# A gated recurrence of 512 steps: the product with wh_W from three bf16 parts, r and z in one fp32 product

## The chip, the cores and the metric

The kernel runs on one core of a Trainium2 chip. The metric is the time of one execution on the device in microseconds; where several runs are named, their median. PE (TensorE), VectorE (DVE), ScalarE (ACT), GpSimd (POOL) and SyncE (SP) are the engines of that core; PEld is TensorE's loading of weights, which can overlap its matmuls.

## What is computed

The input x has 8 sequences of 512 steps with 512 values, h0 is (8, 512). With T = 512 steps in order:

```python
def step(h, x_t):
    fused = sigmoid(concatenate([x_t, h], -1) @ w_W + w_b)
    hidden_state, output_state = split(fused, 2, -1)          # r, z
    memory_state = x_t @ wx_W + wx_b + hidden_state * (h @ wh_W + wh_b)
    h_new = output_state * h + (1.0 - output_state) * tanh(memory_state)
    return h_new, h_new
_, hs = scan(step, h0, swapaxes(x, 0, 1))
return x + swapaxes(hs, 0, 1)
```

Everything is fp32. The products with x_t do not depend on h; the three products with h (r's and z's lower half of w_W, and wh_W, each 512 x 512) do, so a step cannot begin before the step ahead of it has given h.

## The kernel before, in words

**Layout.** The 512 hidden values lie as 4 chunks k of 128 partitions. Chunks 0 and 1 are half A of the state, chunks 2 and 3 half B; a tile hT of one half holds both its chunks. For a product, the state of a chunk is the stationary operand (32 columns: 4 steps of a group times 8 sequences, of which 8 are this step's) and the weights are the moving one. The output's 128 partitions are four groups j of 32 rows: a matmul with `to[32 * j : 32 * j + 32]` uses a quarter of the array's columns, and four of them, one for each j, can run side by side. One matmul call in fp32 leaves two LDWEIGHTS and two MATMUL records.

**Banks of a step.** Three PSUM tiles, double buffered by groups of GS = 4 steps: A (192 columns: h, z and r of half a), B (128: r and h of half b) and C (64: z of half b). "Half a" and "half b" are here halves of each group's 128 output columns, which become half A and half B of the new state. TensorE takes the steps' products in the order `ORDER` (line 27; the digit is the chunk k of the state), each item being four matmuls (line 344). Behind them come 7 matmuls of the x side (line 351, `take(later, 7)`): products of x with wx for later groups, 192 columns each, which do not depend on the recurrence. The first index j is turned by 7 each step (`turn`, line 352), so that the four groups j, which get 2, 2, 2 and 1 of the seven, take turns in having one less. In the first five steps the x side is `prefill` (384 columns a matmul); at the end of the run, from about step 501, it is used up.

**VectorE and ScalarE, in program order of a step** (lines 426 to 451): VectorE transposes 32 x 32 blocks out of PSUM, ScalarE takes sigmoid and tanh, and scans do the arithmetic. `turn_r(0)`, `turn_h(0)`, `turn_z(0)`, then `memory(0, 0)` and `memory(0, 1)`: for each chunk a scan of 16 elements, which makes r * (h wh_W + wh_b) + x-part, and a tanh. Then `turn_r(1)`, `turn_h(1)`, `update(0, 0)`, `turn_z(1)`, `update(0, 1)`: the update is a scan of 24 elements (three slots for each sequence: h, tanh, new h), and its output in slot 2 is the new state that the next step's A0 (chunk 0) and A1 (chunk 1) load as weights. Then `memory(1, ...)`, `update(1, ...)`, whose output A2, A3 and so on load, and a ScalarE copy of each half's new state into slot 0 of the tile. Each engine works in this order; a wait blocks what stands behind it on that engine. `idle` (lines 400 and 504) are tiny memsets on VectorE.

**Beside it**: `turn_x` transposes the x-part of the memory state, `spread` and other ScalarE copies prefill banks A, B and C with the x-parts, POOL makes sums of x (`x_sum`) and adds x to the new state for the output (`add`, two of them a step), SP loads x and stores the output in blocks of 16 steps.

**Start.** SP loads wx (4 x 768 KB), wa (4 x 384 KB) and wb (1152 and 384 KB). VectorE makes weight sums `tw` for the x side (line 277), two of them ahead of step 0.

The next lines are the functions that the change touches.

## Time and profile before

| | |
|---|---|
| three runs | 1674.72 us median, 1672.09 to 1675.40 |
| profiled execution, its span | 1670.8 us |
| PE busy | 1659.0 us (99%), 56238 records |
| PEld busy | 1637.5 us (98%), 56238 records |
| VectorE busy | 1090.5 us (65%), 9387 instructions |
| ScalarE busy | 1029.9 us (62%), 5822 instructions |
| POOL busy | 301.9 us (18%), 1281 instructions |
| DMA | 31.40 MB, mean 19 GB/s |

How to read the lines that follow. Busy shares are unions of record times; matmuls are pipelined, so that records of one engine overlap, and a record is longer than the time after which the next one can start. A line of the timeline has start and length in us, the engine, the source line, the operation, output tile <- input tiles, the shape (partitions x elements; 128*32 is 128 rows by 32 columns of the array) and how many records were merged; in brackets is the idle time before it and what ended it. A line of groups ends in busy us, mean ns of one | idle time before, with its releasers. A line of stretches has, for a window in us, its length, the busy time and the number of instructions of PE, PEld, VectorE, ScalarE and POOL, the granted clock of TensorE, the DMA share and GB/s. Every matmul has source line L188, that of a helper, so groups are told apart by their tiles.

### The profile page before, as it was taken

Reading aid. Unit: us, or ns where it says so; the run is one execution under the profiler, and the core shown is the slowest. Engines: PE = TensorE matmul, PEld = TensorE weight load, DVE = VectorE, ACT = ScalarE, POOL = GpSimd, SP = SyncE. Lnnn points to the kernel's source line nnn. Section 1 sums busy time; section 2 is a strip of 40 time slices with the busy share of each in tenths; the row PEclk is TensorE's granted clock in tenths of the full one; section 3 lists DMA queues with packets and bytes.
Section 4 is the critical chain, followed back from the end, with each engine's and each line's share of the span. In section 5 each row is a group of like instructions: output and inputs, shape, how many; then the busy total and the mean of one; then the engine's idle time right before and its main releaser. Section 6 shows DMA issues by size and latency. Waiting matters only on the chain.

```text
span 1670.8 us, 129875 instructions
## 1 busy us (share of the span) xinstructions
PE 1659.0 (99%) x56238; PEld 1637.5 (98%) x56238; DVE 1090.5 (65%) x9387; ACT 1029.9 (62%) x5822; POOL 301.9 (18%) x1281
## 2 busy tenths in 40 slices
PE   8999999999999999999999999999999999999998
PEld 5999999999999999999999999999999999999997
DVE  6666666666666666666666666666666666666666
ACT  3666666666666666666666666666666666666665
POOL 1111111111111111111111111111111111111111
PEclk9999999999999999999999999999999999999999
DMA  4000000000000000000000000000000000000000
GB/s 179 17 5 17 18 18 17 17 6 17 17 18 18 5 17 18 17 17 5 18 17 17 18 11 12 18 17 17 18 5 17 17 18 17 5 17 12 11 12 10
DMA packets 11525, 31.40 MB, mean 19 GB/s; under 512 B 1220, under 2 KB 1732, under 8 KB 10824
## 3 DMA queue, kind: packets, MB, share of 16 engines
q1 hardware_dynamic: 10800, 22.94, 4.0%
q8 instruction: 440, 7.21, 1.8%
q14 instruction: 133, 1.09, 0.2%
q10 hardware_dynamic: 152, 0.16, 0.0%
HBM read 14.70 MB, written 8.39 MB: 14 GB/s over the span
## 4 chain that ended last, share of the span: by engine, by line
PE 98%; DVE 1%; DMA 0%; issue 0%; ACT 0%
PE A L188 44%; PE B L188 23%; PE xp L188 20%; PE C L188 12%; DMA rows<-in_bias_dram 0%; DVE tr L374 0%; DVE m L358 0%; DVE tz L374 0%; DVE md1B L390 0%; DVE md1A L390 0%; DVE hTA L358 0%; DVE bias L203 0%; ACT hTB L216 0%; ACT xp L224 0%; DVE rows L120 0%
## 5 line engine op out<-in xcount | busy, mean ns | idle before, releaser
L188 PE MATMUL A<-wa,hTA 128*32 128x192 f32 x8176 | 638.2, 329 | 2.3 <-DVE hTA L358 2.3
L188 PE MATMUL B<-wb,hTA 128*32 128x128 f32 x8192 | 573.8, 273 | 0.0
L188 PE MATMUL A<-wa,hTB 128*32 128x192 f32 x8176 | 507.4, 326 | 0.5 <-DVE hTB L358 0.5
L188 PEld LDWEIGHTS B<-wb,hTA 128*32 128x32 f32 x8192 | 471.2, 122 | 1.4 <-issue 0.2
L374 DVE STREAM_TRANSPOSE tr<-A 128x64 f32<-128x64 f32 x511 | 127.7, 250 | 463.5 <-PE A L188 463.5
L188 PE MATMUL B<-wb,hTB 128*32 128x128 f32 x8192 | 398.9, 273 | 0.0
L188 PEld LDWEIGHTS A<-wa,hTA 128*32 128x32 f32 x8176 | 385.4, 123 | 7.6 <-DVE hTA L358 4.0
L188 PEld LDWEIGHTS A<-wa,hTB 128*32 128x32 f32 x8176 | 372.9, 122 | 2.7 <-DVE hTB L358 0.8
L216 ACT ACTIVATE md0A<-tr 128x16 f32<-128x16 f32 x512 | 112.3, 219 | 421.0 <-DVE tr L374 421.0
L507 POOL TENSOR_TENSOR ot<-xin,hTB 128x16 f32<-128x16 f32 x503 | 125.9, 250 | 1324.5 <-DVE hTB L358 1314.0
L188 PEld LDWEIGHTS B<-wb,hTB 128*32 128x32 f32 x8192 | 321.5, 122 | 0.1
L188 PE MATMUL C<-wb,hTA 128*32 128x64 f32 x8192 | 289.4, 219 | 0.0
L188 PE MATMUL C<-wb,hTB 128*32 128x64 f32 x8192 | 288.9, 220 | 0.2 <-issue 0.2
L188 PEld LDWEIGHTS C<-wb,hTA 128*32 128x32 f32 x8192 | 266.7, 122 | 0.0
L188 PE MATMUL xp<-tw,sx 128*32 128x192 f32 x2976 | 237.2, 326 | 0.1
L188 PEld LDWEIGHTS C<-wb,hTB 128*32 128x32 f32 x8192 | 229.2, 123 | 0.4 <-issue 0.4
L358 DVE TENSOR_TENSOR_SCAN hTB<-hd0B,hTB 128x24 f32<-128x24 f32 x1024 | 157.8, 195 | 101.0 <-ACT hTB L216 99.8
L358 DVE TENSOR_TENSOR_SCAN hTA<-hd0A,hTA 128x24 f32<-128x24 f32 x1024 | 191.0, 187 | 0.0
L188 PE MATMUL xp<-wx,xin 128*32 128x192 f32 (+1 forms) x2048 | 182.4, 331 | 0.7 <-issue 0.5
L216 ACT ACTIVATE hd0B<-tz 128x16 f32<-128x16 f32 x512 | 115.2, 225 | 93.7 <-DVE tz L374 93.7
L216 ACT ACTIVATE hTB<-hTB 128x16 f32<-128x16 f32 x512 | 120.5, 235 | 79.8 <-DVE hTB L358 72.3
L216 ACT ACTIVATE hTB<-m 128x8 f32<-128x8 f32 x1024 | 160.6, 206 | 0.0
(92 smaller groups left out, 2489.6 us busy)
## 6 DMA issues: line engine op xcount, KB each, us to landing
xin<-in_x_dram SPq DMA_DIRECT2D x31, 256.0 KB, 3.5
out_dram<-ot SPq DMA_DIRECT2D x31, 256.0 KB, 2.2
wx<-in_wx_dram SPq DMA_DIRECT2D x4, 768.0 KB, 7.1
wa<-in_wa_dram SPq DMA_DIRECT2D x4, 384.0 KB, 8.9
wb<-in_wb_dram SPq DMA_DIRECT2D x1, 1152.0 KB
wb<-in_wb_dram SPq DMA_DIRECT2D x1, 384.0 KB, 11.1
out_dram<-ot SPq DMA_DIRECT2D x1, 192.0 KB, 3.9
head<-in_xh_dram ACTq DMA_DIRECT2D x1, 144.0 KB, 5.0
```

The lines of the kernel that those rows point to most:

```text
L188: nc.tensor.matmul(out_, lhsT, rhs, start=start, stop=False, skip_group_check=True)
L216: inst = nc.scalar.activation(out_, in_, func, **kw).ins
L358: return nc.vector.tensor_tensor_scan(*[t_[:, :, c_].rearrange("p n c s -> p (n c s)") for t_ in (out_, d0, d1)], 0.0, ALU.mult, ALU.add,).ins
L374: inst = nc.vector.transpose(t_.rearrange("p c n -> p (c n)"), raw[n][hf]).ins
L507: return engine.tensor_tensor(ot[:, t, 2 * hf : 2 * hf + 2, :].rearrange("p c n -> p n c"), x_of(c, slice(2 * hf, 2 * hf + 2), t, 1).rearr ...
```

## The change

Banks C and the h columns of A and B go. `ps["A"]` and `ps["B"]` now have 128 columns each, z and r of half a and of half b, from one fp32 product each with `wrz` (256 columns a chunk and group).

The product with wh_W is made in bf16. At the start `parts` holds three bf16 parts of each of wh_W's chunks (rounded value, rounded rest, rest). In every step the new state of each half is cut into three bf16 parts too: part 0 is the upper half of the fp32 word that ScalarE copies (`copies_of`), parts 1 and 2 come from two VectorE subtractions (`split`). The parts of one chunk, 8 sequences each, are 24 neighbouring rows of the tile's slot 0 and are loaded together as 24 stationary columns, read as bf16 at the tile's step of 12 bytes. Items a and b of the order stand for 12 matmuls each (3 parts of the weights x 4 groups j) of 64 moving columns, into PSUM tiles `hps` that start anew each step; rows 24 to 31 of each group keep the bias wh_b. So h @ wh_W + wh_b lies in four rows of 8, which are summed, together with the x-part, inside the memory scan: it now has NE = 5 elements for each sequence and runs once for both chunks of a half, 2 x 8 x 5 = 80 elements. There is one tanh for a half instead of two.

The order on VectorE becomes turn_rz(0), turn_h(0), memory(0), turn_rz(1), turn_h(1), update(0) (two scans), memory(1), split(0), update(1), split(1). The copies of a half follow its update directly on ScalarE. The `idle` memsets are gone. The order on TensorE ends with b0 to b3, and the x side behind it.

```diff
-ORDER = "A0 B0 A1 A2 A3 B1 B2 B3 C0 C1 C2 C3"
-FIRST = "A0 x A1 x A2 x A3 B0 B1 B2 B3 C0 C1 C2 C3"
-BANKS = {"A": 192, "B": 128, "C": 64}
+ORDER = "A0 B0 A1 B1 A2 A3 a0 a1 a2 a3 B2 B3 b0 b1 b2 b3"
+FIRST = "a0 a1 a2 a3 b0 b1 b2 b3 A0 x A1 x A2 x A3 B0 B1 B2 B3"
+ROWS = 96
+NE = 5
...
+    whole = const.tile([P, NQ, NQ, 128], F32, name="whole")
+    for k in range(NQ):
+        nc.sync.dma_start(out=whole[:, k], in_=wh_d[k])
+    wrz = const.tile([P, NQ, NQ, 256], F32, name="wrz")
+    for k in range(NQ):
+        nc.sync.dma_start(out=wrz[:, k], in_=wrz_d[k])
+    parts = const.tile([P, NQ, 3, NQ, 128], BF16, name="parts")
...
+    hT = [[const.tile([P, 2, ROWS, 3], F32, name=f"hT{n}{i}") for i in range(NH)] for n in "AB"]
+    def upper(t_):
+        flat = t_.rearrange("p c r s -> p (c r s)").bitcast(BF16)
+        return flat.rearrange("p (c r s e) -> p c r s e", c=2, r=ROWS, s=3)[:, :, :, :, 1]
+    hi = [[upper(t_) for t_ in ts] for ts in hT]
+    md0 = [[const.tile([P, GS, 2, B, NE], F32, name=f"md0{n}{i}") for i in range(2)] for n in "AB"]
+    md1 = [[const.tile([P, GS, 2, B, NE], F32, name=f"md1{n}{i}") for i in range(2)] for n in "AB"]
...
+    def part_of(hf, i, n, of=hT):
+        s = B * (i % GS) + 32 + B * n
+        return of[hf][i % NH][:, :, s : s + B, 0]
+    def split(hf, i):
+        s = B * (i % GS)
+        nc.vector.tensor_tensor(
+            part_of(hf, i, 1), state(hf, i), hi[hf][i % NH][:, :, s : s + B, 2], ALU.subtract
+        )
+        nc.vector.tensor_tensor(
+            part_of(hf, i, 2), part_of(hf, i, 1), part_of(hf, i, 1, hi), ALU.subtract
+        )
+    def copies_of(hf, i):
+        s = B * (i % GS)
+        to = hT[hf][i % NH].rearrange("p c (d r) s -> p d c r s", r=32)[:, :2, :, s : s + B, 0]
+        return to, state(hf, i).rearrange("p (o c) b -> p o c b", o=1).broadcast_to([P, 2, 2, B])
...
+    hps = [psum.tile([P, HU], F32, name=f"hh{n}") for n in "AB"]
...
+    for k in range(NQ):
+        nc.scalar.copy(parts[:, k, 0], whole[:, k])
+        nc.vector.tensor_tensor(whole[:, k], whole[:, k], parts[:, k, 0], ALU.subtract)
+        nc.scalar.copy(parts[:, k, 1], whole[:, k])
+        nc.vector.tensor_tensor(parts[:, k, 2], whole[:, k], parts[:, k, 1], ALU.subtract)
...
+            if bank in "AB":
+                hs = hT[k // 2][i % NH][:, k % 2, :32, 2]
+                to = ps[bank] if i or hf else xps[0][:, XP["A"]]
+                for j in range(NQ):
+                    j = (j + turn[0]) % NQ
+                    mm(to[32 * j : 32 * j + 32], hs, wrz[:, k, j, 128 * hf : 128 * hf + 128])
+                continue
+            hs = hi[k // 2][i % NH][:, k % 2, 32 + B * s : 56 + B * s, 0]
+            for q in range(3):
+                for j in range(NQ):
+                    j = (j + turn[0]) % NQ
+                    mm(
+                        hps[hf][32 * j : 32 * j + 24],
+                        hs,
+                        parts[:, k, q, j, HU * hf : HU * hf + HU],
+                        start=(k == 0 and q == 0),
+                    )
...
+        def memory(hf):
+            m = work.tile([P, 2, B, NE], F32, tag=f"m{hf}", name=f"m{hf}_{i}")
+            scan(*[t_.rearrange("p c b e -> p (c b e)") for t_ in (m, md0[hf][g % 2][:, s], md1[hf][g % 2][:, s])])
+            act(("n", hf, i % NH), state(hf, i, 1), m[:, :, :, NE - 1], AF.Tanh)
...
+        gates(0, turn_rz(0))
+        turn_h(0)
+        memory(0)
+        gates(1, turn_rz(1))
+        turn_h(1)
+        update(0)
+        if i < T - 1:
+            act(("h", 0, (i + 1) % NH), *copies_of(0, i + 1), AF.Copy)
...
+        memory(1)
+        if i < T - 1:
+            split(0, i + 1)
+        update(1)
+        if i < T - 1:
+            act(("h", 1, (i + 1) % NH), *copies_of(1, i + 1), AF.Copy)
+            split(1, i + 1)
```

More of the change, by code (lines that the diff above doesn't have):

```diff
@@ L18 @@
 HU = 64
-DVE_FILL = 23
-IDLE = 3
+DVE_FILL = 24
 LAST = 4
 SYNC = mybir.DependencyInfo(mybir.DependencyClass.Sync, mybir.DependencyReason.DATA)
-ORDER = "A0 B0 A1 A2 A3 B1 B2 B3 C0 C1 C2 C3"
-FIRST = "A0 x A1 x A2 x A3 B0 B1 B2 B3 C0 C1 C2 C3"
-BANKS = {"A": 192, "B": 128, "C": 64}
+ORDER = "A0 B0 A1 B1 A2 A3 a0 a1 a2 a3 B2 B3 b0 b1 b2 b3"
+FIRST = "a0 a1 a2 a3 b0 b1 b2 b3 A0 x A1 x A2 x A3 B0 B1 B2 B3"
+ROWS = 96
+NE = 5
 HALF = 192
@@ L36 @@
 GA, DE = (1, slice(64, 256)), (1, slice(256, 448))
-XP = {"A": slice(0, 192), "X": slice(192, 320), "C": slice(320, 384), "B": slice(384, 512)}
+XP = {"A": slice(64, 192), "X": slice(192, 320), "B": slice(320, 448)}
 @with_exitstack
@@ L47, in tile_cond_rnn_residual @@
     wx_d: bass.AP,
-    wa_d: bass.AP,
-    wb_d: bass.AP,
-    wb3_d: bass.AP,
+    wh_d: bass.AP,
+    wrz_d: bass.AP,
     bias_d: bass.AP,
@@ L125, in tile_cond_rnn_residual @@
         nc.sync.dma_start(out=wx[:, k], in_=wx_d[k])
-    wa = const.tile([P, NQ, NQ, 192], F32, name="wa")
+    whole = const.tile([P, NQ, NQ, 128], F32, name="whole")
     for k in range(NQ):
-        nc.sync.dma_start(out=wa[:, k], in_=wa_d[k])
-    wb = const.tile([P, NQ, NQ, 192], F32, name="wb")
-    nc.sync.dma_start(out=wb[:, :3], in_=wb_d)
-    nc.sync.dma_start(out=wb[:, 3], in_=wb3_d)
-    def wh(bank, k, j):
-        return wa[:, k, j] if bank == "A" else wb[:, k, j, {"C": slice(0, 64), "B": slice(64, 192)}[bank]]
+        nc.sync.dma_start(out=whole[:, k], in_=wh_d[k])
[3 more added lines that the diff above has]
+    parts = const.tile([P, NQ, 3, NQ, 128], BF16, name="parts")
     load_x(0, 1)
-    def pair(n, name, rows, slots):
-        return const.tile([P, 2, rows, slots], F32, name=name).rearrange("p c n s -> p n c s")
     NH = 2 * GS
-    hT = [[pair(n, f"hT{n}{i}", 32, 3) for i in range(NH)] for n in "AB"]
-    md0 = [[pair(n, f"md0{n}{i}", 32, 2) for i in range(2)] for n in "AB"]
-    md1 = [[pair(n, f"md1{n}{i}", 32, 2) for i in range(2)] for n in "AB"]
-    hd0 = [[pair(n, f"hd0{n}{i}", B, 3) for i in range(2)] for n in "AB"]
+    hT = [[const.tile([P, 2, ROWS, 3], F32, name=f"hT{n}{i}") for i in range(NH)] for n in "AB"]
[5 more added lines that the diff above has]
+    md1 = [[const.tile([P, GS, 2, B, NE], F32, name=f"md1{n}{i}") for i in range(2)] for n in "AB"]
+    hd0 = [[const.tile([P, 2, B, 3], F32, name=f"hd0{n}{i}") for i in range(2)] for n in "AB"]
     zeros = const.tile([P, 512], F32, name="zeros")
@@ L161, in tile_cond_rnn_residual @@
     nc.scalar.activation(const.tile([P, 1], F32, name="table"), zeros[:, :1], AF.Sigmoid)
-    for n, t_ in enumerate(hd0[0] + hd0[1] + md0[0] + md0[1] + hT[0] + hT[1]):
+    for n, t_ in enumerate(hd0[0] + hd0[1] + [t_[:, :, :32] for t_ in hT[0] + hT[1]]):
         (nc.vector if n < DVE_FILL else nc.gpsimd).memset(t_, 0.0)
@@ L165, in tile_cond_rnn_residual @@
         nc.gpsimd.memset(t_[:, :, :, 1], -1.0)
-    idle = const.tile([P, IDLE], F32, name="idle")
+    for t_ in md0[0] + md0[1]:
+        nc.gpsimd.memset(t_, 1.0)
+        nc.gpsimd.memset(t_[:, :, :, :, 0], 0.0)
     tw = [const.tile([P, 2, NQ, HALF], F32, name=f"tw{n}") for n in range(4)]
@@ L177, in state @@
         s = i % GS
-        return hT[hf][i % NH][:, B * s : B * s + B, :, slot]
+        return hT[hf][i % NH][:, :, B * s : B * s + B, slot]
+    def part_of(hf, i, n, of=hT):
[13 more added lines that the diff above has]
+        return to, state(hf, i).rearrange("p (o c) b -> p o c b", o=1).broadcast_to([P, 2, 2, B])
     ctx.enter_context(tc.manual_schedule())
-    banks = [
-        {n: psum.tile([P, w], F32, name=f"{n}{q}") for n, w in BANKS.items()}
-        for q in range(2)
-    ]
+    banks = [{n: psum.tile([P, 128], F32, name=f"{n}{q}") for n in "AB"} for q in range(2)]
+    hps = [psum.tile([P, HU], F32, name=f"hh{n}") for n in "AB"]
     xps = [psum.tile([P, 512], F32, name=f"xp{q}") for q in range(2)]
@@ L203, in tile_cond_rnn_residual @@
     nc.vector.tensor_copy(bias, xps[0])
-    for hf in range(2):
-        for slot in (0, 2):
-            nc.vector.tensor_copy(
-                state(hf, 0, slot), hin[:, 2 * hf : 2 * hf + 2].rearrange("p c b -> p b c")
-            )
+    for hf, c0 in ((0, 0), (1, 448)):
+        nc.vector.tensor_copy(hps[hf], bias[:, c0 : c0 + HU])
+        nc.vector.tensor_copy(state(hf, 0), hin[:, 2 * hf : 2 * hf + 2])
+        nc.scalar.activation(*copies_of(hf, 0), AF.Copy)
+        split(hf, 0)
+    for k in range(NQ):
[3 more added lines that the diff above has]
+        nc.vector.tensor_tensor(parts[:, k, 2], whole[:, k], parts[:, k, 1], ALU.subtract)
     turn = [0]
@@ L255, in turn_x @@
         c0 = XP["X"].start + 32 * e
-        nc.vector.transpose(md1[e // 2][g % 2][:, :, e % 2, 1], part(g, c0, c0 + 32))
+        nc.vector.transpose(md1[e // 2][g % 2][:, :, e % 2, :, NE - 1], part(g, c0, c0 + 32))
     def reg(r):
@@ L323, in tile_cond_rnn_residual @@
     weight_sum(2)
-    spread(0, "BCA")
+    spread(0, "BA")
     for e in range(NQ):
@@ L342, in tile_cond_rnn_residual @@
             bank, k = n[0], int(n[1])
-            hs = hT[k // 2][i % NH][:, :, k % 2, 2]
-            for j in range(NQ):
-                j = (j + turn[0]) % NQ
-                to = ps[bank] if i or bank != "A" else xps[0][:, XP["A"]]
-                mm(to[32 * j : 32 * j + 32, :], hs, wh(bank, k, j))
+            hf = "ABab".index(bank) % 2
+            if bank in "AB":
[15 more added lines that the diff above has]
+                    )
         if i < 5:
@@ L354, in tile_cond_rnn_residual @@
         rows = slice(B * s, B * s + B)
-        def scan(c_, out_, d0, d1):
-            return nc.vector.tensor_tensor_scan(
-                *[t_[:, :, c_].rearrange("p n c s -> p (n c s)") for t_ in (out_, d0, d1)],
-                0.0,
-                ALU.mult,
-                ALU.add,
-            ).ins
-        pa = ps["A"] if i else xps[0][:, XP["A"]]
-        raw = {
-            "h": (pa[:, :HU], ps["B"][:, HU:]),
-            "z": (pa[:, HU : 2 * HU], ps["C"]),
-            "r": (pa[:, 2 * HU :], ps["B"][:, :HU]),
-        }
@@ L372, in turned @@
-        def turned(n, hf):
-            t_ = work.tile([P, 2, 32], F32, tag=f"t{n}{hf}", name=f"t{n}{hf}_{i}")
-            inst = nc.vector.transpose(t_.rearrange("p c n -> p (c n)"), raw[n][hf]).ins
-            return t_[:, :, rows], inst
-        r_done = [None, None]
-        h_done = [None, None]
-        def turn_r(hf):
-            tr, _ = turned("r", hf)
-            r_done[hf] = act(
-                ("r", hf, g % 2, s),
-                md0[hf][g % 2][:, rows, :, 1].rearrange("p n c -> p c n"),
-                tr,
-                AF.Sigmoid,
-            )
@@ L389, in turn_h, with scan, turn_rz @@
-        def turn_h(hf):
-            inst = nc.vector.transpose(
-                md1[hf][g % 2][:, :, :, 0].rearrange("p n c -> p c n"), raw["h"][hf]
-            ).ins
-            h_done[hf] = inst
+        def scan(out_, d0, d1):
+            return nc.vector.tensor_tensor_scan(out_, d0, d1, 0.0, ALU.mult, ALU.add).ins
+        rz = (ps["A"] if i else xps[0][:, XP["A"]], ps["B"])
+        def turn_rz(hf):
+            t_ = work.tile([P, 2, 2, 32], F32, tag=f"rz{hf}", name=f"rz{hf}_{i}")
+            inst = nc.vector.transpose(t_.rearrange("p g c n -> p (g c n)"), rz[hf]).ins
@@ L394, in turn_h @@
             if hf == 0 and i + 1 - NH in pool_done:
                 tc.add_manual_dep(inst, pool_done[i + 1 - NH].name, SYNC)
-        def turn_z(hf):
-            tz, _ = turned("z", hf)
-            if hf == 0:
-                inst = nc.vector.memset(idle[:, IDLE - 1 :], 0.0).ins
-                tc.add_manual_dep(inst, h_done[0].name, SYNC)
-            act(
-                ("zc", hf, i % 2),
-                hd0[hf][i % 2][:, :, :, 2].rearrange("p n c -> p c n"),
-                tz,
-                AF.Sigmoid,
-                scale=-1.0,
-            )
@@ L410, in tile_cond_rnn_residual @@
-        ms = [
-            work.tile([P, 2, B, 2], F32, tag=f"m{hf}", name=f"m{hf}_{i}").rearrange("p c n s -> p n c s")
-            for hf in range(2)
-        ]
-        def memory(hf, q):
-            c_ = slice(q, q + 1)
-            scan(c_, ms[hf], md0[hf][g % 2][:, rows], md1[hf][g % 2][:, rows])
-            act(("n", hf, q, i % NH), state(hf, i, 1)[:, :, c_], ms[hf][:, :, c_, 1], AF.Tanh)
-        def update(hf, q):
-            s1 = (i + 1) % GS
-            new = hT[hf][(i + 1) % NH][:, B * s1 : B * s1 + B]
-            return scan(slice(q, q + 1), new, hd0[hf][i % 2], hT[hf][i % NH][:, rows])
@@ L426, in tile_cond_rnn_residual, with gates, turn_h @@
-        turn_r(0)
+            return t_
+        def gates(hf, t_):
+            act(("r", hf, g % 2, s), md0[hf][g % 2][:, s, :, :, NE - 1], t_[:, 1, :, rows], AF.Sigmoid)
+            act(("zc", hf, i % 2), hd0[hf][i % 2][:, :, :, 2], t_[:, 0, :, rows], AF.Sigmoid, scale=-1.0)
+        def turn_h(hf):
+            nc.vector.transpose(
+                md1[hf][g % 2][:, s].rearrange("p c b e -> p c e b")[:, :, :4], hps[hf]
+            )
+        def memory(hf):
+            m = work.tile([P, 2, B, NE], F32, tag=f"m{hf}", name=f"m{hf}_{i}")
+            scan(*[t_.rearrange("p c b e -> p (c b e)") for t_ in (m, md0[hf][g % 2][:, s], md1[hf][g % 2][:, s])])
+            act(("n", hf, i % NH), state(hf, i, 1), m[:, :, :, NE - 1], AF.Tanh)
@@ new lines, in update @@
+        def update(hf):
+            s1 = B * ((i + 1) % GS)
+            for q in range(2):
+                scan(
+                    *[
+                        t_.rearrange("p b e -> p (b e)")
+                        for t_ in (
+                            hT[hf][(i + 1) % NH][:, q, s1 : s1 + B],
+                            hd0[hf][i % 2][:, q],
+                            hT[hf][i % NH][:, q, rows],
+                        )
+                    ]
+                )
+        gates(0, turn_rz(0))
@@ L427, in tile_cond_rnn_residual @@
         turn_h(0)
-        turn_z(0)
-        memory(0, 0)
-        memory(0, 1)
-        turn_r(1)
+        memory(0)
+        gates(1, turn_rz(1))
         turn_h(1)
-        update(0, 0)
-        turn_z(1)
-        tc.add_manual_dep(update(0, 1), r_done[1].name, SYNC)
+        update(0)
+        if i < T - 1:
+            act(("h", 0, (i + 1) % NH), *copies_of(0, i + 1), AF.Copy)
         if i == 0:
@@ L440, in tile_cond_rnn_residual @@
             nc.gpsimd.tensor_tensor(
-                ot[:, t, :2, :].rearrange("p c n -> p n c"),
-                x_of(c, slice(0, 2), t, 1).rearrange("p c n -> p n c"),
+                ot[:, t, :2, :],
+                x_of(c, slice(0, 2), t, 1),
                 state(0, T),
@@ L445, in tile_cond_rnn_residual @@
             )
-        memory(1, 0)
-        memory(1, 1)
-        update(1, 0)
-        update(1, 1)
-        for hf in range(2):
-            act(("h", hf, (i + 1) % NH), state(hf, i + 1, 0), state(hf, i + 1), AF.Copy)
+        memory(1)
[5 more added lines that the diff above has]
+            split(1, i + 1)
         if i < 3:
@@ L467, in tile_cond_rnn_residual @@
                 nc.scalar.copy(reg(GA), reg(BE))
-        elif u == 1:
-            spread(2 * o + 1, "C")
         elif u == 2 and o == 0:
@@ L487, in tile_cond_rnn_residual @@
         elif u == 5 and nxt:
-            spread(2 * o + 2, "C")
+            pass
             if two:
@@ L503, in tile_cond_rnn_residual @@
             nc.gpsimd.tensor_tensor(step_bias, bias[:, BE[1]], bias[:, AL[1]], ALU.subtract)
-        for n in range(IDLE - 1):
-            nc.vector.memset(idle[:, n : n + 1], 0.0)
         def add(hf, engine):
             return engine.tensor_tensor(
-                ot[:, t, 2 * hf : 2 * hf + 2, :].rearrange("p c n -> p n c"),
-                x_of(c, slice(2 * hf, 2 * hf + 2), t, 1).rearrange("p c n -> p n c"),
+                ot[:, t, 2 * hf : 2 * hf + 2, :],
+                x_of(c, slice(2 * hf, 2 * hf + 2), t, 1),
                 state(hf, i + 1),
@@ L575 @@
     wx_d = chunks(cat((z[:D], half_a), (r[:D], half_a), (wxm, both), (z[:D], half_b), (r[:D], half_b)))
-    wa_d = chunks(cat((whm, half_a), (z[D:], half_a), (r[D:], half_a)))
-    wb = units(cat((z[D:], half_b), (r[D:], half_b), (whm, half_b)))
-    wb_d, wb3_d = c_(wb[:, :3]), c_(wb[:, 3])
+    wh_d = chunks(quads(whm))
+    wrz_d = chunks(cat((z[D:], half_a), (r[D:], half_a), (z[D:], half_b), (r[D:], half_b)))
     rb, zb = wb_[:512], wb_[512:]
@@ L592 @@
     for name, a in (
-        ("x", xd), ("xh", xh_d), ("wx", wx_d), ("wa", wa_d), ("wb", wb_d), ("wb3", wb3_d), ("bias", bias_d),
+        ("x", xd), ("xh", xh_d), ("wx", wx_d), ("wh", wh_d), ("wrz", wrz_d), ("bias", bias_d),
     ):
```

## The prediction

> **What bounds the kernel now.** First the page's head, its chain of waits and a stretch of the middle, for whether TensorE ever waits; then TensorE in order of time.

> ```profile
> span 1670.8 us, 129875 instructions
> PE 98%; DVE 1%; DMA 0%; issue 0%; ACT 0%
> 400.00:800.00 400.00, 399.82 (x13682) 398.24 (x13677) 261.18 (x2268) 249.76 (x1417) 72.69 (x310) 1.00 0.05 16
> ```

> The chain is nearly all TensorE, at the full granted clock (1.00). An fp32 product leaves two MATMUL records, so a step has 2 x (16 A + 16 B + 16 C + 7 of the x side) = 110; 13682 records in 400 us make a step of **3.216 us**. That a busy PE is not a PE at its peak shows in one of the last steps, which have no x side left:

> ```profile
> 1660.94 0.55 PE L188 MATMUL A<-wa,hTA 128*32 128x192 f32 x8 [0.24 <-DVE hTA L358]
> 1661.31 0.40 PE L188 MATMUL B<-wb,hTA 128*32 128x128 f32 x8
> ...
> 1661.85 0.83 PE L188 MATMUL A<-wa,hTB 128*32 128x192 f32 x16
> 1662.50 0.40 PE L188 MATMUL B<-wb,hTA 128*32 128x128 f32 x8
> 1662.72 0.62 PE L188 MATMUL B<-wb,hTB 128*32 128x128 f32 x16
> 1663.16 0.41 PE L188 MATMUL C<-wb,hTA 128*32 128x64 f32 x16
> 1663.38 0.41 PE L188 MATMUL C<-wb,hTB 128*32 128x64 f32 x16
> 1664.02 0.55 PE L188 MATMUL A<-wa,hTA 128*32 128x192 f32 x8 [0.24 <-DVE hTA L358]
> ...
> 1663.48 0.23 DVE L374 STREAM_TRANSPOSE tr<-B 128x64 f32<-128x64 f32 x1
> 1663.63 0.21 DVE L390 STREAM_TRANSPOSE md1B<-B 128x64 f32<-128x64 f32 x1
> 1663.77 0.20 DVE L358 TENSOR_TENSOR_SCAN hTA<-hd0A,hTA 128x24 f32<-128x24 f32 x1
> ...
> 1664.03 0.17 DVE L358 TENSOR_TENSOR_SCAN hTA<-hd0A,hTA 128x24 f32<-128x24 f32 x1
> 1664.12 0.25 DVE L358 TENSOR_TENSOR_SCAN m<-md0B,md1B 128x16 f32<-128x16 f32 x2
> 1664.56 0.31 DVE L358 TENSOR_TENSOR_SCAN hTB<-hd0B,hTB 128x24 f32<-128x24 f32 x2 [0.20 <-ACT hTB L216]
> ```

> Read the first column as a clock. Each group of 32 output rows (j = 0 to 3) works through its own quarter of the records; I call four records side by side a round. 64 columns of C take (1663.38 - 1663.16)/4, about 0.056 us a round, 128 of B (1663.16 - 1662.72)/4 = 0.11 (I use 0.109), 192 of A (1662.50 - 1661.85)/4 = 0.163, and the x side has A's shape. So a step costs A 8 x 0.163, B 8 x 0.109, C 8 x 0.056, and the x side 7/4 x 2 x 0.163 = 0.570: **3.19 us of streaming** in the 3.216.

> The other limit is a loop. B ends at 1663.16; its last result is turned (tr, md1B), the scan at 1663.77 makes the first chunk of the new half A, and A0 starts streaming at 1664.02 + 0.04 (its block is 0.37 long instead of 0.326: the weights come late). That is 0.90 us, of which A0's first weights are the last 0.04. C (0.448) and the x side cover it. The seven x products are spread over four groups, so each step three groups have two (0.652) and one, in turn, has a single one (0.326). A group with two goes from B's end to A0 in 0.448 + 0.652 = 1.100; one with a single product would need 0.774 and waits about 0.86 instead. Carried over four steps this is (3 x 1.10 + 0.86)/4 = 1.04; with A and B (2.176), 3.216. That is the measured step, so I use the same bookkeeping after the change.

> **The change, part by part.** A step loses C (0.448) and A's third 64 columns: r and z are now A and B of 128 columns each, 16 rounds x 0.109 = 1.744 us. The product with wh_W becomes 96 bf16 matmuls of 64 columns (a and b), 24 rounds of length p. The x side stays 0.570. Streaming is 2.314 + 24p.

> **p is the unknown.** The trace has no column-tiled bf16 matmul. Its bounds:

> ```profile
> L188 PEld LDWEIGHTS C<-wb,hTA 128*32 128x32 f32 x8192 | 266.7, 122 | 0.0
> L188 PEld LDWEIGHTS xp<-tw,sx 128*32 128x32 f32 x2976 | 137.1, 110 | 1.3 <-issue 0.4
> L188 PE MATMUL C<-wb,hTA 128*32 128x64 f32 x8192 | 289.4, 219 | 0.0
> ...
> 2.31 0.26 PE L188 MATMUL C<-none 128*128 128x64 bf16 x1
> ...
> 2.52 0.31 PE L188 MATMUL B<-none 128*128 128x128 bf16 x1
> ...
> 802.73 0.12 PEld L188 LDWEIGHTS C<-wb,hTB 128*32 128x32 f32 x1
> 802.73 0.26 PE L188 MATMUL C<-wb,hTB 128*32 128x64 f32 x1
> ```

> - Below: a bf16 record streams one pass where an fp32 record streams two, so half of C's 53.5 ns plus its fixed 2.5: **29 ns**. [...]
> - Above: C's own round, **56 ns**, the densest in the trace.
> - Between lies the weight load, which C's round hides and 27 ns of streaming may not. At 802.73 a load and its matmul start together, and the matmul takes 262 ns (0.26) instead of 219: 32 columns need 43 ns before streaming starts; A0's 0.37 says 40. I take 42. In a busy group the next load starts as the previous matmul starts, so p is at least the load. Now 24 columns are loaded, of the same tile at the same 12-byte stride. If all scales, 42 x 24/32 = 31.5. If only what the stride adds (122 - 110 = 12 ns against the contiguous load) scales, 39. With 1.5 ns between the starts: 33 to 40.5. Nearest is this strided load, and part of a load is surely fixed, so I take **p = 36**, 24p = 0.864.

> [...]

> **The loop after the change.** The last bank is now b, and only the x side covers what follows: the 0.448 of C is gone from there.

> ```profile
> 801.91 0.33 PE L188 MATMUL A<-wa,hTB 128*32 128x192 f32 x1
> 802.27 0.25 DVE L374 STREAM_TRANSPOSE tr<-A 128x64 f32<-128x64 f32 x1 [1.02 <-PE A L188]
> ```

> From the end of b's streaming: the record's tail 219 - 56 = 0.163; to VectorE 0.037 (the last A matmul ends at 802.24, tr starts at 802.27); turn_h(1) to the scan 0.13 (1663.63 to 1663.77); scan 0.20; scan to A0's record 0.05 (1663.97 to 1664.02); load 0.04: **0.62 us**. The turn_rz(1) ahead of it depends on B3, 12 rounds earlier, and is done. A group with two x products passes in 0.652, the one with a single product waits to 0.62: mean (3 x 0.652 + 0.62)/4 = 0.644. Step = 1.744 + 0.864 + 0.644 = **3.252 us**, against 3.216: +0.036.

> Edits that I cost at nothing, and their cover, counted from b's end, with a start of A0 at 0.62:
> - The 80-element scan replaces two of 16. 24 elements cost 187 to 195 ns, 16 cost 167 to 181, so 8 more cost 6 to 28; 80 cost 0.24 to 0.39. Half B: scan starts at 0.2 + 0.13 + 0.125 + 0.09 = 0.54, ends at 0.78 to 0.93, then 0.06 + tanh 0.21 + 0.05 + update 0.20 + 0.05, so A2 can load at 1.30 to 1.50 (the waits as above, 0.03 to 0.06 between VectorE and ACT). It is due at 0.62 + 4 x 0.218 = 1.49. Covered, without room at the far end.
> - split(1), two VectorE subtractions behind update(1) (I take 0.19 each, a tensor-tensor of 16 elements in this trace), and the ACT copy (0.235) beside it: the second update ends 1.43 to 1.63, splits by 1.81 to 2.01, plus 0.05. a2 is due at 1.49 + 0.436 + 6p = 2.14. Queued behind a2's wait on TensorE is all of a2 to b3 and the x side. split(0) has over 0.3 more.
> - Half A's turn_h, scan and tanh run under B2, B3 and b (0.87). VectorE loses two transposes, two scans and three memsets, and gains four subtractions.

> ```profile
> L358 DVE TENSOR_TENSOR_SCAN hTA<-hd0A,hTA 128x24 f32<-128x24 f32 x1024 | 191.0, 187 | 0.0
> L358 DVE TENSOR_TENSOR_SCAN hTB<-hd0B,hTB 128x24 f32<-128x24 f32 x1024 | 157.8, 195 | 101.0 <-ACT hTB L216 99.8 <-ACT hTA L216 1.1
> L358 DVE TENSOR_TENSOR_SCAN m<-md0A,md1A 128x16 f32<-128x16 f32 x1024 | 142.1, 181 | 4.2
> L358 DVE TENSOR_TENSOR_SCAN m<-md0B,md1B 128x16 f32<-128x16 f32 x1024 | 128.1, 167 | 0.0
> L507 DVE TENSOR_TENSOR ot<-xin,hTB 128x16 f32<-128x16 f32 x1 | 0.2, 188 | 0.1
> L216 ACT ACTIVATE hTB<-hTB 128x16 f32<-128x16 f32 x512 | 120.5, 235 | 79.8 <-DVE hTB L358 72.3 <-DVE idle L505 0.8
> L216 ACT ACTIVATE hTB<-m 128x8 f32<-128x8 f32 x1024 | 160.6, 206 | 0.0
> L224 ACT COPY xp<-bias 128x512 f32<-128x512 f32 x3 | 1.8, 587 | 5.0 <-DVE bias L203 5.0
> L277 DVE TENSOR_TENSOR tw<-wx,tw 128x384 f32<-128x384 f32 x8 | 4.1, 518 | 0.0
> 11.31 1.76 DVE L277 TENSOR_TENSOR tw<-wx 128x1536 f32<-128x1536 f32 x1 [0.35 <-DMA wx<-in_wx_dram]
> 18.29 0.25 DVE L374 STREAM_TRANSPOSE tr<-xp 128x64 f32<-128x64 f32 x1 [3.62 <-PE xp L188]
> ```

> **The start.** The weights are the same 3 MB, wh_W first in the SP queue. Four chunks are cut into parts: copy 0.59, subtraction about 0.65 (518 ns for 384 elements), copy 0.59, in order on ACT, so 1.9 us a chunk and 7.7 us from about 12.3 (an estimate: the last of wx lands by 11.31, wh_W's first chunk is next). The weight sums (2 x 1.76) stand behind that on VectorE, so the first turn, at 18.29 now, comes near 24.7. Step 0 has then less left to do behind it (its b is done first): **+5 us**, between +2 and +7.

> **Sum**, against the span: 496 steps with this x side x 0.036 = 17.9; the last 11 without x, 1.744 + 0.864 + 0.62 = 3.23 against 3.08, +1.6; the first 5, with x products of 384 columns, -0.1; start +5. **+24 us on 1670.8**. The median of the runs is 1674.7, 0.2% over the span; I add the 24 to it: **1699 us**, 1.5% slower. Each ns of p is 24 x 512 = 12.3 us; the change breaks even at p = 34.0.

> **Rivals.**
> 1. *A bf16 load takes half an fp32 one* (half the bytes) and p is the 29 ns of streaming. For: fp32 streams at half rate. Against: at this stride the bytes are not read in a row. -86 + 24: **1613 us**, loop still deciding.
> 2. *TensorE can't be fed*: 348 instead of 220 instructions a step, four load-matmul pairs in 29 to 36 ns where C has them in 56. Decides once a pair costs over 8.5 ns. For: nothing denser is sustained in the trace. Against: nothing there asked for more, as C is bound by its columns. At 56: 24 x 0.020 x 512 = +246: **1945 us**.
> [...]

> ```profile
> 24.85 0.52 DVE L277 TENSOR_TENSOR tw<-wx,tw 128x384 f32<-128x384 f32 x1
> 24.90 0.57 POOL L507 TENSOR_TENSOR ot<-head,hTB 128x16 f32<-128x16 f32 x1 [2.76 <-DVE hTB L358]
> 25.43 0.24 POOL L507 TENSOR_TENSOR ot<-head,hTA 128x16 f32<-128x16 f32 x1
> ```

> 4. *Loads don't overlap a running matmul of the same group* in bf16: p = 27 + 34 = 61, +307 on the forecast: **2006 us**. Against: C's round of 56 is its 53.5 of streaming plus 2.5, with the load inside. [...]

> **How the numbers follow.** Forecast (p 33 to 40.5: 1662 to 1754) 0.43; rival 1 0.34; rival 2 0.09; rival 3 0.09; rival 4 0.02; else 0.03. Two executions of this kernel can be told apart from about 0.2%. Faster: rival 1 and the low end of the forecast, 0.38. Same: p within 0.3 of 34.0, 0.05. Slower: 0.57. The range runs from rival 1 (1613, less the start's spread) over rival 3 to p = 44 (all of the load fixed, 1797): 1608 to 1800.

> **What would show it.** Right: rounds of a and b near 36 ns with matmul starts spaced by their loads; A0's load 0.05 behind the scan of hTA every step; a step of 3.25; the first turn near 24.7. Wrong: rounds of 29 or over 42; waits of a2 on VectorE; a step that differs from 2.39 + 24 times the round measured.

## The result and the profile after

The changed kernel takes 2593.18 us (median of 4 runs, 2586.68 to 2599.77) against 1674.17 us for the kernel before (4 runs, 1672.09 to 1675.40): ratio 1.550, 95% interval 1.547 to 1.553. The forecast was 1699 us. The direction was right, the size was not: the time lies far outside the range.

The head of the page after, its queue of instruction transfers, its chain of waits and a stretch of its middle (a "packet" is one transfer of a queue):

```profile
span 2592.2 us, 194785 instructions
PE 1910.9 (74%) x89004; PEld 1670.4 (64%) x89004; DVE 1557.4 (60%) x7856; ACT 962.8 (37%) x4678; POOL 302.6 (12%) x1288
q8 instruction: 698, 11.44, 1.8%
PE 71%; issue 25%; DVE 2%; ACT 1%; DMA 0%; POOL 0%; SPq 0%; DVEq 0%; ACTq 0%; POOLq 0%
800.00:1200.00 400.00, 295.14 (x13879) 259.51 (x13867) 240.12 (x1218) 148.97 (x727) 47.00 (x200) 1.00 0.04 11
```

TensorE is busy 74% of the time instead of 99%, at the same full clock (1.00), and a quarter of the chain is "issue": time in which the engine waited for nothing that the profile shows. It is not data that is late. VectorE has 2% of the chain, and no engine is full. Strangest is the number of records: TensorE does 13879 in these 400 us, and the kernel before did 13682 in its 400 us. The step has grown from 220 instructions to 349 (348 loads and matmuls, as the prediction counted, and some of TensorE's sequencer, 736 in the whole trace), and **the number of instructions per microsecond has nearly stayed the same**.

The timeline of TensorE shows where the idle time stands:

```profile
1180.68 0.42 PE L208 MATMUL hhB<-parts,hTB 128*24 128x64 bf16 x23
1182.74 0.35 PE L208 MATMUL xp<-wx,xin 128*32 128x192 f32 x1 [1.65 <-issue]
...
1185.69 0.19 PE L208 MATMUL hhB<-parts,hTA 128*24 128x64 bf16 x1
1186.30 0.40 PE L208 MATMUL hhB<-parts,hTA 128*24 128x64 bf16 x22 [0.40 <-issue]
...
1188.74 0.35 PE L208 MATMUL hhA<-parts,hTA 128*24 128x64 bf16 x18
1189.60 0.26 PE L208 MATMUL hhA<-parts,hTA 128*24 128x64 bf16 x6 [0.51 <-issue]
...
1191.96 0.39 PE L208 MATMUL A<-wrz,hTA 128*32 128x128 f32 x4
1193.45 0.32 PE L208 MATMUL A<-wrz,hTA 128*32 128x128 f32 x2 [1.10 <-issue]
```

The stalls end at 1182.74, 1186.30, 1189.60 and 1193.45: every 3.3 to 3.9 us, in the x side, in b, in a, in A, and in the middle of items, where nothing new is needed. Their places have no relation to the step (5.0 us). In the view of the DMA queues, the stretch from 1180 to 1192 us, cut into 40 slices of 0.3 us, gives them a companion:

```profile
GB/s 55 0 0 0 0 0 0 0 0 0 0 0 0 55 0 0 0 0 0 0 0 0 0 27 55 0 0 0 0 0 0 0 0 0 0 0 55 0 0 0
q8 instruction: 4, 0.07, 2.2%
```

Four packets of queue 8 (55 GB/s, 16 KB in a slice; the 27 is half as much for another queue), in slices 0, 13, 24 and 36, which by the trace start at 1180.16, 1183.91, 1187.41 and 1190.82 us: the last three 1.1 to 1.2 us behind the end of a stall. The page's total gives the size: 11.44 MB in 698 packets is 16,384 bytes each, and 178,008 TensorE records (89,004 twice) over 698 is 255, or 256 with the sequencer's 736. **A packet is a block of 256 of TensorE's instructions.** Counting TensorE's instructions through the trace:

```
                                            before    after
starts more than 0.33 us apart (from 100 us)    15      685
of these at instruction 193 of a block of 256    4      673
mean time from packet to packet, us          3.737    3.675
```

673 of 685 stalls stand at one place of the 256, whatever instruction that is. All 673 end 1.19 to 1.61 us behind the landing of a packet, while these spaces from start to start run from 0.34 to 2.66 us: it is the landing that lets TensorE go on. So TensorE runs out of instructions once per block, and gets a block every 3.675 us, 14.4 ns an instruction; 349 of them take 5.01 us. By the spans and the first turns (28.62 us in the row below) a step takes (2592.2 - 28.6)/512 = 5.01 us.

The one row of the page before that held this was not among those that the prediction read:

```profile
q8 instruction: 440, 7.21, 1.8%
```

1670.8/440 = 3.80 us a packet. The kernel before, with its full TensorE, was within some 2% of the same limit (220 instructions at 14.4 ns are 3.16 us, its step was 3.216), and nothing else that is shown of its page tells it.

What the change does inside a step was close to the forecast. An early step of after, ahead of the first stall at place 193, which ends at 39.94 us (the x products have 384 columns there); a stretch between two stalls, which end at 1203.76 and 1207.33; and the start on VectorE:

```profile
34.82 0.43 PE L208 MATMUL A<-wrz,hTA 128*32 128x128 f32 x8
...
37.01 0.41 PE L208 MATMUL hhB<-parts,hTA 128*24 128x64 bf16 x23
...
37.46 1.49 PE L208 MATMUL xp<-wx,xin 128*32 128x384 f32 x15
38.74 0.43 PE L208 MATMUL A<-wrz,hTA 128*32 128x128 f32 x8
...
1204.62 0.42 PE L208 MATMUL hhB<-parts,hTA 128*24 128x64 bf16 x24
1204.83 0.42 PE L208 MATMUL hhB<-parts,hTB 128*24 128x64 bf16 x24
1205.08 0.66 PE L208 MATMUL xp<-wx,sx 128*32 128x192 f32 x10
...
1205.71 0.44 PE L208 MATMUL A<-wrz,hTA 128*32 128x128 f32 x8
```

```profile
20.49 3.42 DVE L302 TENSOR_TENSOR tw<-wx 128x1536 f32<-128x1536 f32 x2
...
28.62 0.32 DVE L402 STREAM_TRANSPOSE rz<-xp 128x128 f32<-128x128 f32 x1 [4.27 <-PE xp L208]
```

Six rounds of b (24 records) take 1204.83 - 1204.62 = 0.21 us, 35 ns a round.

### The profile page after: what moved, and what is told of

Its sections match the earlier page's. It is cut to its first block, busy times and chain, and to the rows that moved or that the text cites. A ratio compares the mean times of both kernels' runs of the same rounds, so it can differ in the third digit from the quotient of the medians.

```text
span 2592.2 us, 194785 instructions
## 1 busy us (share of the span) xinstructions
PE 1910.9 (74%) x89004; PEld 1670.4 (64%) x89004; DVE 1557.4 (60%) x7856; ACT 962.8 (37%) x4678; POOL 302.6 (12%) x1288
## 3 DMA queue, kind: packets, MB, share of 16 engines
q8 instruction: 698, 11.44, 1.8%
q14 instruction: 125, 1.02, 0.1%
## 4 chain that ended last, share of the span: by engine, by line
PE 71%; issue 25%; DVE 2%; ACT 1%; DMA 0%; POOL 0%; SPq 0%; DVEq 0%; ACTq 0%; POOLq 0%
PE A L208 19%; PE B L208 18%; PE xp L208 13%; PE hhA L208 11%; PE hhB L208 10%; DVE m L396 1%; DMA whole<-in_wh_dram 0%; DVE hTB L396 0%; DVE md1A L412 0%; DVE md1B L412 0%; DVE hTA L192 0%; DVE rz L402 0%; ACT hTA L241 0%; POOL ot L512 0%; DVE hTB L189 0%
## 5 line engine op out<-in xcount | busy, mean ns | idle before, releaser
L208 PEld LDWEIGHTS <-hTA 128*24 128x24 bf16 x24576 | 467.5, 118 | 158.2 <-issue 155.3
L208 PE MATMUL A<-wrz,hTA 128*32 128x128 f32 x8176 | 483.0, 280 | 78.1 <-issue 67.5
L208 PEld LDWEIGHTS <-hTB 128*24 128x24 bf16 x24576 | 385.8, 118 | 237.7 <-issue 232.1
L208 PE MATMUL B<-wrz,hTA 128*32 128x128 f32 x8192 | 470.4, 275 | 67.9 <-issue 67.9
L208 PE MATMUL A<-wrz,hTB 128*32 128x128 f32 x8176 | 384.9, 278 | 37.3 <-issue 33.1
L208 PE MATMUL B<-wrz,hTB 128*32 128x128 f32 x8192 | 359.0, 279 | 37.9 <-issue 37.8
L208 PEld LDWEIGHTS A<-wrz,hTA 128*32 128x32 f32 x8176 | 273.0, 125 | 164.2 <-issue 76.6
L208 PEld LDWEIGHTS B<-wrz,hTA 128*32 128x32 f32 x8192 | 308.9, 122 | 87.8 <-issue 87.7
L208 PE MATMUL hhA<-parts,hTB 128*24 128x64 bf16 x12288 | 248.3, 203 | 81.9 <-issue 80.0
L208 PE MATMUL hhA<-parts,hTA 128*24 128x64 bf16 x12288 | 263.7, 201 | 59.6 <-issue 59.4
L208 PEld LDWEIGHTS A<-wrz,hTB 128*32 128x32 f32 x8176 | 260.3, 124 | 69.9 <-issue 47.2
```

Of the source, the lines that this page charges most:

```text
L208: nc.tensor.matmul(out_, lhsT, rhs, start=start, stop=False, skip_group_check=True)
```

## The experiments

Two theories. **Supply**: TensorE gets 256 instructions in about 3.68 us, whatever they are; a step costs its instructions by 14.4 ns, where its own streaming or loop is not longer. **Pairs**: the dense bf16 loads and matmuls are what is slow, about 28 ns for a pair of them, and fp32 work is as before. The first four kernels were meant to tell these apart. Runs 1 to 8 are one execution each; 9 has four. Runs 5 to 8 were taken on another chip than 1 to 4, where the kernel before took 1682.03 us (span 1679.6) and not 1673.88.

**1. No bf16 at all** (from the kernel after; a and b are one fp32 product of 64 columns with wrz in place of the three-part product, so the product with wh_W is left out): 285 instructions a step.

```diff
-            hs = hi[k // 2][i % NH][:, k % 2, 32 + B * s : 56 + B * s, 0]
-            for q in range(3):
-                for j in range(NQ):
...
+            hs = hT[k // 2][i % NH][:, k % 2, 32 + B * s : 56 + B * s, 0]
+            for j in range(NQ):
+                j = (j + turn[0]) % NQ
+                mm(hps[hf][32 * j : 32 * j + 24], hs, wrz[:, k, j, HU * hf : HU * hf + HU], start=(k == 0))
```

> The kernel after with no bf16 matmul in its steps: a and b are single fp32 products of 64 columns, by a part of the r and z weights (the three-part product with wh_W is left out, so the output is not the reference's). Streaming is that of the kernel before (3.19 us a step), and 128 + 128 + 28 = 285 instructions. Theory 1: 4.10 us a step, about 2125 us. Theory 2: no bf16 pair, so streaming or the loop decide: 1.744 + 0.448 x 2 / 2 + 0.644 = 2.84 to 3.2 us, 1500 to 1700 us.

2124.81 us. Its instruction queue and its chain:

```profile
q8 instruction: 570, 9.34, 1.8%
PE 86%; issue 10%; DVE 2%; DMA 0%; ACT 0%; SPq 0%; DVEq 0%; ACTq 0%
```

Without a single bf16 product in the step the stalls remain (466 of 479 at place 193), at 2122.7/570 = 3.72 us a packet. The pair theory falls here.

**2. The bf16 work untouched, fewer fp32 instructions** (from after; A and B as one fp32 product of 256 columns, the same columns in half the instructions): 285 a step.

```diff
-ORDER = "A0 B0 A1 B1 A2 A3 a0 a1 a2 a3 B2 B3 b0 b1 b2 b3"
+ORDER = "R0 R1 R2 R3 a0 a1 a2 a3 b0 b1 b2 b3"
...
+            if bank == "R":
...
+                    mm(rzs[g % 2][32 * j : 32 * j + 32], hs, wrz[:, k, j, :])
```

> The kernel after with A and B as one product of 256 columns: the same streaming and the same 96 bf16 matmuls, 64 TensorE instructions a step less (285 for 349). Theory 1: 4.10 us a step, about 2125 us. Theory 2: the bf16 pairs are all there, 5.06 us a step or more, about 2590 us.

2136.50 us. The same number of instructions as in 1 and nearly the same time, from a kernel that has all 96 bf16 matmuls and half the fp32 ones of r and z; the pair theory had 2590. It is the less clean of the two: 17% of its chain is VectorE's, and 312 of its 606 gaps stand at place 193.

**3. a and b merged** (from after; one bf16 product of 128 columns, 48 matmuls for 96): 253 a step.

```diff
+ORDER = "A0 B0 A1 B1 A2 A3 h0 h1 h2 h3 B2 B3"
...
+                    mm(hh[32 * j : 32 * j + 24], hs, parts[:, k, q, j, :], start=(k == 0 and q == 0))
```

> The kernel after with a and b as one bf16 product of 128 columns, ahead of B2 and B3: 48 bf16 pairs instead of 96, 253 instructions. Theory 1: 3.64 us a step, about 1890 us. Theory 2: 48 x 0.028 + 1.744 + 0.87 (the loop from B's end, with the turn of r and z in it) = 3.95 us, about 2050 us. Without either, the loop: 1.744 + 12 x 0.056 + 0.87 = 3.29 us, 1710 us.

1899.22 us, near the supply's number. It tells less than the two above: 28% of its chain is VectorE's, only 68 of its 520 gaps stand at place 193, and run 9 shows that its loop alone comes to about 3.57 us a step, close under the 3.65 that 253 instructions take at this kernel's 3.69 us a block.

**4. The kernel before with 64 more instructions**, bare bf16 weight loads of a constant, two before each matmul of A and B:

```diff
+                for _ in range(extra(bank, k)):
+                    nc.tensor.ldweights(none[:, :32], tile_position=(0, 32 * j))
```

> The kernel before with 64 more TensorE instructions in each step: two bf16 loads of 32 columns ahead of each fp32 matmul of A and B, of weights that no matmul uses (64 loads; A and B have 32 calls). The array has room for them behind rounds of 0.109 and 0.163 us. Theory 1 (instruction supply: TensorE gets 256 instructions per 3.68 us, 69.6 a us, whatever they are): 284 instructions a step, 4.08 us, about 2110 us in all, with stalls put down to issue once per 256 instructions. Theory 2 (a bf16 load-matmul pair of a quarter of the array costs 28 ns to issue, and fp32 is not concerned): no pairs are added, 1675 to 1720 us.

2225.91 us, 116 over the supply's number, and not for its reason alone:

```profile
PE 2211.1 (99%) x56238; PEld 2196.5 (99%) x89006; DVE 1143.6 (51%) x9387; ACT 1091.6 (49%) x5822; POOL 303.0 (14%) x1281
q8 instruction: 568, 9.31, 1.7%
```

```profile
L188 PE MATMUL C<-wb,hTA 128*32 128x64 f32 x8192 | 404.0, 230 | 0.0
```

TensorE is 99% busy and has no stalls; C's records, which have no added loads beside them, cover 404 us in place of 289. So the added loads slowed the array itself (a C record takes 230 ns in place of 219), and 2223.6/568 = 3.91 us a packet is longer than the supply takes. The run excludes neither theory, and the next two replace it.

**5 and 6. The kernel before with more matmuls on the same columns**: each of A's products as one of 128 and one of 64 columns, for all chunks (284 instructions), and, with `and k == 0` in the condition, for chunk 0 alone (236). The streaming is unchanged: 0.109 + 0.056 against 0.163 a round.

```diff
+                if i and bank == "A":
+                    for cols in (slice(0, 128), slice(128, 192)):
+                        mm(to[32 * j : 32 * j + 32, cols], hs, wh(bank, k, j)[:, cols])
+                    continue
```

> The kernel before with each fp32 product of A (192 columns) as two, of 128 and 64 columns: the same streaming (rounds of 0.109 and 0.056 for 0.163) and nothing else changed, but 64 more TensorE instructions a step, 284. All loads belong to a matmul, unlike in loads64, where the array itself slowed down. Theory 1 (256 instructions per 3.68 us): 4.08 us a step, 2100 to 2130 us, with stalls of issue once per 256 instructions. Theory 2 (bf16 pairs at 28 ns): 1675 to 1700 us.

> The same for A0 alone: 16 more instructions, 236 a step. Theory 1: 3.39 us a step, 1755 to 1775 us. Theory 2: 1675 to 1685 us.

2141.34 and 1783.30 us, each some 10 us over its upper bound. TensorE in the first of them, and the heads of the page in the second:

```profile
1001.98 0.66 PE L188 MATMUL xp<-wx,xin 128*32 128x192 f32 x10
1003.44 0.35 PE L188 MATMUL xp<-wx,xin 128*32 128x192 f32 x1 [0.80 <-issue]
...
1005.99 0.39 PE L188 MATMUL C<-wb,hTB 128*32 128x64 f32 x12
1007.46 0.26 PE L188 MATMUL C<-wb,hTB 128*32 128x64 f32 x1 [1.08 <-issue]
```

```profile
span 1780.8 us, 138051 instructions
PE 1738.9 (98%) x60326; PEld 1656.3 (93%) x60326; DVE 1108.1 (62%) x9387; ACT 1033.1 (58%) x5822; POOL 302.0 (17%) x1281
```

The kernel before, given 64 more instructions and no more work, shows the stalls of the kernel after (539 of 540 at place 193). And 16 more are enough: 110 us on the span of the profile before (1670.8), 101 on that of the kernel before taken beside it (1679.6), while TensorE still looks 98% busy. The excess over the expectation is in the size of the supply: a packet comes every 3.72 us here, not 3.68.

**7. The third part of wh_W left out** (from after: `for q in range(2)` in the step): 285 instructions, two thirds of the bf16 work.

> The kernel after without the third part of wh_W in its steps (that part of the product is left out): 64 bf16 matmuls a step, 285 instructions, 0.28 us less streaming than rz256 and 0.3 less than fp32_h, which have 285 too. Theory 1: as these two, 4.09 us a step, 2115 to 2140 us. Theory 2: 2.39 + 64 x 0.028 = 4.18 us, 2170 us.

2167.31 us: 27 over the upper bound of the supply theory, and at the number of the pair theory. Alone it would speak for pairs, which runs 1, 2 and 5 exclude. Its trace has 543 of 558 gaps at place 193 and a packet every 3.76 us, and 285 instructions at that rate are 4.19 us a step; (2165.2 - 28.6)/512 = 4.17 were measured. So the supply decides here too, and its time was put too short. Part of the 2% over the kernel after lies in the packet itself, which takes 1.11 us in the mean against 1.06; runs 5 and 6, of the same chip, have 1.09, runs 1 and 2 have 1.07 and 1.06. So the difference may be the chip's; that was not tried.

**8. Both merged** (2 and 3 together): 189 instructions a step, the same columns.

> The kernel after with both merged: r and z in one product of 256 columns, a and b in one of 128, 189 instructions a step. Theory 1: supply needs only 2.72 us, so stalls at one place in 256 go, and the loop decides: 1.744 + 12 x 0.056 + 1.3 to 1.5 (from the end of h over turn, scan, tanh and update to the next load, 1.52 in the run wide) = 3.7 to 3.95 us, 1920 to 2050 us. Theory 2: another 0.67 us, 2260 to 2390 us.

2058.11 us, 8 over the upper end, with 0 of 495 gaps at place 193 and 2056.0/378 = 5.44 us a packet. TensorE now waits for data instead:

```profile
1006.82 0.83 PE L210 MATMUL xp<-tw,sx 128*32 128x192 f32 x14
1008.34 0.87 PE L210 MATMUL R<-wrz,hTA 128*32 128x256 f32 x12 [0.69 <-DVE hTA L399]
```

Once few enough, the instructions set nothing, and the loop through VectorE, of which an order without B2 and B3 at the end covers little, decides.

**9. Merged as in 3, two parts as in 7**: 221 instructions, one more than the kernel before.

> The merged product of a and b (one bf16 product of 128 columns) with the third part of wh_W left out as well: 253 - 32 = 221 TensorE instructions a step, one more than the kernel before. Supply theory (256 instructions in 3.68 us): 3.18 us a step at least, so the loop decides. From the trace of the merged kernel: h's rounds stream 0.055 us (six in 0.33), so a step streams 1.744 + 8 x 0.055 + 0.57 = 2.75; from h's end to the next A0 lie 1.52 us, of which B2, B3 and the x side fill about 1.0, so 0.5 of waiting on VectorE: 3.25 to 3.30 a step, plus about 25 us of start: 1690 to 1720 us, with the idle time of TensorE given to VectorE and next to none to issue. Rival (dense bf16 pairs themselves cost about 28 ns each, 64 of them a step): 64 x 0.028 = 1.79 in place of 0.44: 4.1 to 4.6 a step, 2120 to 2370 us.

1746.15 us (1744.38 to 1747.92; before 1671.69; ratio 1.044, 1.042 to 1.046), 26 over the upper end. The waits are the loop's, as expected:

```profile
L209 PE MATMUL A<-wrz,hTA 128*32 128x128 f32 x8176 | 430.8, 282 | 134.1 <-DVE hTA L392 133.1
L209 PE MATMUL B<-wrz,hTA 128*32 128x128 f32 x8192 | 411.7, 273 | 0.0
```

The step is (1745.0 - 28.6)/512 = 3.35 us, taking the start of the kernel after, against 3.25 to 3.30 expected, and the start was put 4 us short. With 4 more rounds of h at 0.055 us it is the 3.57 used in 3. This kernel still has 32 bf16 pairs a step (the expectation counted 64, which are its loads and matmuls, so its rival's number is too high), and streams its h rounds of four in 0.055 us, 14 ns a pair and not 28.

All of it in one table, from the pages (records are PE and PEld; the gaps are counted as above):

| kernel | records | packets | span us | us per packet | gaps at place 193 |
|---|---|---|---|---|---|
| before | 112476 | 440 | 1670.8 | 3.80 | 4 of 15 |
| 6, A0 split | 120652 | 472 | 1780.8 | 3.77 | 119 of 130 |
| 3, a and b merged | 128856 | 506 | 1897.1 | 3.75 | 68 of 520 |
| 5, A split | 145180 | 567 | 2138.2 | 3.77 | 539 of 540 |
| 7, two parts | 145240 | 570 | 2165.2 | 3.80 | 543 of 558 |
| 1, no bf16 | 145240 | 570 | 2122.7 | 3.72 | 466 of 479 |
| 2, A and B merged | 145300 | 570 | 2134.4 | 3.74 | 312 of 606 |
| after | 178008 | 698 | 2592.2 | 3.71 | 673 of 685 |
| 9, merged, two parts | 112472 | 442 | 1745.0 | 3.95 | 17 of 491 |
| 4, bare loads | 145244 | 568 | 2223.6 | 3.91 | 1 of 12 |
| 8, both merged | 96148 | 378 | 2056.0 | 5.44 | 0 of 495 |

The first eight differ by a factor of 1.55 in time and by 2.4% in time per packet. The kernel before is among them although its array holds it, because the array is only just slower than the supply (3.216 us a step against 3.16). The last three, whose array or loop is slower still, lie above. None of the nine, nor the kernel after, is faster than the kernel before.

## Why the prediction was wrong, step by step

- **p, the unknown of the sum: the number right, its reason not shown.** 36 ns chosen, 35 measured, so rival 1's 29 ns did not come. Streaming alone would allow it: h's rounds of 128 bf16 columns take 0.055 us in run 9, (1004.78 - 1004.56)/4, where 128 fp32 columns take 0.109. That a bf16 record takes half the time of an fp32 one, on which the 29 rests, was the author's estimate until that run: before shows only bf16 matmuls of the start, 0.26 us for 64 columns and 0.31 for 128 (2.31 and 2.52 in the prediction), at a granted clock of 1.00 (2.30 to 2.60 us), so 64 columns more cost about what 64 fp32 columns more do (0.163 - 0.109 us); why the start differs from run 9 no run shows. That the load of 24 strided columns sets the 35 fits, but no run varied the load or its stride alone.
- **The streaming: right.** A, B, a and b were put at 1.744 + 0.864 = 2.61 us; from 34.82 to the x side at 37.44 or 37.46 they take 2.62 to 2.64.
- **The loop behind b: nearly right, and without effect.** From the end of b's streaming (1204.83 + 0.21) to A0's record at 1205.71 are 0.67 us, forecast 0.644. But A0 hardly waits for VectorE (9.4 of its 78.1 us of idle time), because the stalls give the scans the time that they need. For the same reason nothing could come of rival 3, a split(1) that is late for a2, and no run shows its 0.1 to 0.2 us a step: a2 and a3, which read half B, wait on "issue" for 80.0 of 81.9 us. The groups of after:

```profile
L208 PE MATMUL A<-wrz,hTA 128*32 128x128 f32 x8176 | 483.0, 280 | 78.1 <-issue 67.5 <-DVE hTA L396 5.0 <-DVE md1A L281 4.4
...
L208 PE MATMUL hhA<-parts,hTB 128*24 128x64 bf16 x12288 | 248.3, 203 | 81.9 <-issue 80.0 <-ACT hd0A L241 1.9
```

  In the trace of after, POOL's adds also run beside the two subtractions of split(1) in 511 steps, and neither is longer for it: the adds take 224 to 267 ns, the subtractions 180 to 194. The 0.57 us of the add at 24.90 in the prediction come in before only with the eight adds beside a weight sum `tw` (572 to 582 ns); the others take 240 to 264. Whether split(1) would be late in an unstalled step stays open.
- **The start: mis-sized.** The cutting of wh_W ended at 20.6 us (forecast 12.3 + 7.7 = 20.0), and the weight sums behind it at 23.9, as the forecast needs. But VectorE then waited 4.27 us more for TensorE, and the chain of waits of this stretch does not go through the sums:

```profile
19.23 0.62 ACT parts L232
19.84 0.50 ACT xp L249
...
20.39 2.08 PE xp L208 x2
22.46 0.77 PE hhA L208 x25
23.23 0.64 PE hhB L208 x24
23.87 0.58 issue
24.45 4.14 PE xp L208 x56
...
28.62 0.33 DVE rz L402
```

  ScalarE's copy of the bias stands behind the cutting, TensorE's products of zeros wait for that copy, and behind them come the whole of a and b of step 0 and 4.14 us of A and the x side. The forecast has no term for this work of TensorE. 28.6 instead of 24.7: 3.9 us.
- **The failed step: rival 2, "TensorE can't be fed".** It was the right mechanism and was set aside by the wrong measure, so the sum holds streaming and the loop, and no term for the supply of instructions. The prediction compared the spacing inside a round (four pairs in 29 to 36 ns, against C's 56), set its threshold there (8.5 ns a pair) and its price from C's round (1945 us). The array of the kernel after takes pairs at 8.75 ns in its bursts between the stalls, close to that threshold. What is limited is the mean over the step: 14.4 ns for every instruction. "Against: nothing there asked for more, as C is bound by its columns" was true of a round and false of the step, since 220 instructions in 3.216 us is 14.6 ns each. Of the 897 us between the forecast's span (1694.8) and this one (2592.2), the steps hold 893, (5.007 - 3.262) x 512, where 3.262 is the forecast's span less its start over 512; the start holds the rest.
- **The chances.** Slower had 0.57, and came, but through the case that had 0.09, at a time 648 us above that case's own. The range ended at 1800 us, so it did not hold even the rival's 1945.
- **What would show it wrong** named the sign that came: a step (5.01) that differs from 2.39 + 24 times the round measured (2.39 + 0.84 = 3.23).

For this stream of small products the supply is slower than TensorE: the runs give 3.7 us a block of 256, and TensorE could start 256 instructions of a and b in 32 x 35 ns = 1.1 us, an estimate from the rounds measured, of four loads and four matmuls each.

## What to carry to other kernels

Count TensorE's instructions against its instruction queue, not only its busy time: records divided by packets gives the block (after: 178,008/698 = 255), span divided by packets the time of one (2592.2/698 = 3.71 us). In these runs TensorE did not go below 14.4 ns an instruction over many blocks (14.4 to 14.7 where the supply decides), so the fp32 product split into three bf16 parts paid for its number of loads and matmuls, however little each of them streams (35 ns a round of four). A TensorE that was 98 to 99% busy near that rate had next to no room for more instructions (run 6: 7% more of them, 6% more time), and a change there is priced by its number of instructions first and its columns second.
